# Layer 1's weight product for two graphs at a time, from seven half-size products, in a planned four-layer graph kernel

## The chip, the cores and the metric

The kernel runs on one core of one Trainium2 chip. The metric is the device time of one execution in microseconds (us). A core has a matrix engine (PE, whose weight loads are listed apart as PEld), three engines for elementwise work (DVE, ACT and POOL) and DMA queues, most of them fed by SP. Each engine takes its instructions in the order of the program and waits by semaphores for the others.

## The reference, cut to what matters

A batch of 128 graphs, each of 128 nodes with 512 features, passes four layers that share one adjacency matrix. Each layer is added to its input, and the sum is normalised.

```python
# layer 0: max over pairs of a relu, which needs only a row maximum of adj @ x
x = layernorm(x + L0(x, adj, b))
# layer 1: graph attention
h = x @ W                                  # 128x512 by 512x512
s1, s2 = h @ a1, h @ a2
e = leaky_relu(s1[:, :, None] + s2[:, None, :], 0.2) * adj
h_prime = softmax(e, axis=2) @ h
x = layernorm(x + elu(h_prime + beta * h))
# layer 2
x = layernorm(x + (adj @ x) @ W2 + bias2)
# layer 3: attention with 8 heads of 64, masked by adj == 0
q, k, v = x @ Wq + bq, x @ Wk + bk, x @ Wv + bv
x = layernorm(x + softmax(q @ k.T / 8 + mask) @ v)
```

All values are float32.

## The kernel before, in words

Work on a graph is cut into steps, and each step starts with a few matrix products. The names that the profile shows are these. `l0` multiplies by the adjacency (psA). `zT` multiplies the layer's input by the turned attention (ps_zT, L505), and `z` multiplies the result by W (ps_z, L519), which gives h_prime + beta h for one graph: four matrix products of 128x128 by 128x512 (each is two instructions in the trace). `yT` and `y` are the same for layer 2 (L560, L628). `q`, `k` and `v` are layer 3's projections for four graphs (L803), `sc` its scores (L909), `avT` or `av` the weighted sums over the values (L991, L1037).

**Seven products.** `y` takes two graphs together, and `q`, `k`, `v` take four. A product of two blocks by two blocks normally takes eight block products; Winograd's form takes seven and some sums. The sums of the weights are made once on POOL (`weight_sums`, L327). The sums of the other operand are made for each pair on POOL (`y_sums`, L576: four differences of 128x256, tile Ty). The seven products (`l2_seven`, L613) write three PSUM banks: chain, first and pair. The chain bank takes products 0, 2, 4 and 5 on top of each other; after 0, 2 and 4 ACT copies it to SBUF (tile sty, L653), POOL adds the layer's input to the copy (L657), and DVE adds the copy to the first or the pair bank (L665). Product 5 finishes the last quarter (L685). So product 2 waits for the copy after 0, product 4 for the copy after 2, product 5 for the copy after 4.

**Layer 1 before.** `l1_out` (L522) takes one graph. ACT reads the bank and computes relu(-h) and its exponential (L532, L533, tile elu_r); DVE adds the positive part and the layer's input (L536, reading PSUM) and then the exponential (L538); then comes the normalisation (`layernorm`, L351: DVE statistics at L354 and L356, three one-column operations on POOL, and one ACT pass at L365). The attention (`attention`, L458) adds s1 to s2 (L462), takes max(0.2 e, e) (L464), multiplies by adj (L465) and takes the row maximum (L467), all on DVE, and the exponential on ACT (L471). `l0` adds the bias to its maximum and takes the relu on DVE (L409).

**The order.** No scheduler runs later: the class `Plan` (L23) writes out the order while the program is built. It keeps a model of each engine. A step has a place (a priority), a cost on PE, marks that it waits for and buffers that it needs. Whenever PE is free in the model, the ready step with the lowest place is taken. The work behind a step is written as a generator: `yield dve(us)` means that the next instructions take that long on DVE, and the plan puts them into the program in the order in which its model reaches them. HOP (L20) is the model's time for a signal from one engine to the next. `sb_bufs` (L167) holds how many buffers each tile has, and `turns` (L1067) how many graphs a step runs behind `l0`. There are six PSUM banks of 512 columns (mm) and one double bank for scores (sc).

**Turned weights.** Layer 3's softmax weights are turned through a DMA round trip: written out (L376), read back into tile turn_pr (L380), and finished by a DVE transpose (L387). Two buffers (pT) hold the read-back tiles, one of which the weighted sum `avT` reads. The last six graphs are turned on PE (`pT`, L960).

## Time and profile before

| what | value |
|---|---|
| runs | 2715.48 us median of 3 (2715.01 to 2718.81) |
| profiled execution | 2713.79 us |
| its span | 2712.0 us |
| mean granted clock of PE | 0.994 |
| instructions | 45528 |
| DMA traffic | 392.42 MB, mean 145 GB/s |

The profile comes from one execution. Its own time is 1.8 us above the span of its instructions and 1.7 us below the median of the runs. An engine's busy time is the union of its instructions; a group's time is the sum of its own, and neighbours on one engine can overlap by some tens of ns. In rows of groups the columns are: line, engine, operation, output<-inputs, shapes, count, busy us, mean ns of one, and the idle time of the engine just before them with what ended it. In timelines the columns are: start, us, engine, line, operation, tiles, shapes, count. The duration of a matmul includes its way through the array, so the distance between starts says how long PE is taken.

### The profile page before, as it was taken

The numbers are of one execution on the slowest core, as the hardware profiler recorded it, in microseconds if no ns is written. First come the engines' busy times: TensorE is split into PE (matmuls) and PEld (weight loads), VectorE is DVE, ScalarE is ACT, GpSimd is POOL, SyncE is SP. The second block draws the span as 40 slices with busy tenths as digits, with TensorE's granted clock in tenths as the row PEclk, the third lists the DMA queues.
The fourth block names the chain that finished last, engine by engine and source line by source line (L and its number), as shares of the span: only waits on it lengthen the run. The fifth ranks groups of instructions, "written<-read, shape, count | busy, mean of one in ns | idle before, by whom it ended". The sixth has DMA issues, their size and how long they took to land.

```text
span 2712.0 us, 45528 instructions
## 1 busy us (share of the span) xinstructions
PE 2653.9 (98%) x14673; PEld 2076.4 (77%) x14673; DVE 2234.2 (82%) x4417; ACT 1694.8 (62%) x4381; POOL 1710.9 (63%) x2644
## 2 busy tenths in 40 slices
PE   5899999999999999999999999999999999999997
PEld 2677777777777777777777777777777777777786
DVE  7668888888888888888888888888888888888766
ACT  3446666666666666666666666666666666666655
POOL 4745566666666665666665766656666656666655
PEclk8999999999999999999999999999999999999999
DMA  3124545445545454455455455455455445454453
GB/s 126 53 61 142 150 138 161 153 144 153 157 141 152 147 157 154 141 159 158 138 160 158 131 166 151 142 161 154 143 154 159 145 147 159 143 162 137 146 158 128
DMA packets 459807, 392.42 MB, mean 145 GB/s; under 512 B 88752, under 2 KB 376624, under 8 KB 459568
## 3 DMA queue, kind: packets, MB, share of 16 engines
q1 hardware_dynamic: 456464, 383.74, 46.3%
q10 hardware_dynamic: 2976, 5.77, 0.6%
q8 instruction: 115, 1.88, 0.3%
q14 instruction: 124, 1.02, 0.1%
q0 software_dynamic: 128, 0.01, 0.0%
HBM read 218.17 MB, written 171.24 MB: 144 GB/s over the span
## 4 chain that ended last, share of the span: by engine, by line
PE 93%; DVE 2%; POOL 2%; issue 1%; ACT 0%; DMA 0%; SPq 0%; POOLq 0%; DVEq 0%; ACTq 0%
PE ps_z L519 15%; PE ps_k_chain L803 8%; PE ps_q_chain L803 8%; PE ps_y_chain L628 8%; PE ps_v_chain L803 8%; PE ps_sc L909 5%; PE ps_zT L505 4%; PE ps_av L991 4%; PE ps_yT L560 4%; PE ps_k_pair L803 4%; PE ps_y_pair L628 4%; PE ps_v_pair L803 4%; PE ps_q_pair L803 4%; PE psA L404 4%; PE ps_v_first L803 2%; PE ps_q_first L803 2%
## 5 line engine op out<-in xcount | busy, mean ns | idle before, releaser
L519 PE MATMUL ps_z<-w_sb,zT 128*128 128x512 f32 x1024 | 461.4, 593 | 2.1 <-ACT zT L511 2.1
L941 ACT ACTIVATE pr<-pr,nm 128x128 f32<-128x128 f32 x992 | 386.2, 392 | 51.9 <-DVE nm L937 24.6
L519 PEld LDWEIGHTS ps_z<-w_sb,zT 128*128 128x128 f32 x1024 | 193.6, 190 | 195.7 <-issue 183.7
L359 POOL TENSOR_SCALAR ve<-mv 128x1 f32<-128x1 f32 x512 | 118.0, 231 | 331.2 <-DVE mv L356 281.5
L361 POOL TENSOR_TENSOR rstd<-ve,nhalf 128x1 f32<-128x1 f32 x512 | 292.6, 571 | 42.6
L354 DVE BATCH_NORM_STATS2 stats<-xp 128x6 f32<-128x512 f32 x384 | 258.3, 673 | 49.8 <-POOL xp L1017 41.2
L657 POOL TENSOR_TENSOR sty<-sty,x 128x256 f32<-128x256 f32 x192 | 147.7, 769 | 222.4 <-ACT sty L653 203.6
L755 POOL TENSOR_TENSOR x3r<-x3r,bv_bc 128x512 f32<-128x512 f32 x128 | 174.8, 1366 | 162.5 <-DMA x3r<-turn_hbm_x 154.9
L365 ACT ACTIVATE xp<-xp,nmr,rstd 128x512 f32<-128x512 f32 x256 | 206.5, 810 | 94.0 <-POOL nmr L363 82.4
L420 DVE SCALAR_TENSOR_TENSOR x<-x,wa_bc 128x512 f32<-128x512 f32 x256 | 223.9, 875 | 29.0 <-ACT x L365 25.8
L551 POOL TENSOR_TENSOR x<-x,bias_bc 128x512 f32<-128x512 f32 x128 | 165.3, 1291 | 89.9 <-PE ps_yT L560 64.6
L941 ACT ACTIVATION_READ_ACCUMULATOR pr<-pr,nm 128x1 f32 x976 | 184.6, 189 | 0.0
L363 POOL TENSOR_SCALAR nmr<-mv,rstd 128x1 f32<-128x1 f32 x512 | 142.7, 279 | 53.0
L909 PEld LDWEIGHTS ps_sc<-kTh,qTh 64*128 64x128 f32 x2048 | 124.2, 187 | 64.6 <-issue 58.5
L1003 ACT COPY oT<-ps_av 128x512 f32<-128x512 f32 x122 | 133.2, 1092 | 55.3 <-PE ps_av L991 53.2
L1016 POOL TENSOR_TENSOR xp<-xp,rd 128x512 f32<-128x512 f32 x122 | 127.1, 1042 | 62.2 <-DVE xp L391 34.4
L532 ACT ACTIVATE elu_r<-ps_z 128x512 f32<-128x512 f32 x128 | 76.1, 594 | 137.2 <-PE ps_z L519 136.9
L1017 POOL TENSOR_TENSOR xp<-xp,x3r 128x512 f32<-128x512 f32 x122 | 155.6, 1276 | 9.6
L387 DVE STREAM_TRANSPOSE turn_pr<-turn_pr 128x1024 f32<-128x1024 f32 x122 | 150.7, 1235 | 13.1 <-DMA turn_pr<-turn_hbm_pr 12.9
L391 DVE STREAM_TRANSPOSE xTh<-turn_x 128x512 f32<-128x512 f32 x124 | 137.4, 1108 | 25.6 <-DMA turn_x<-turn_hbm_x 25.6
L560 PEld LDWEIGHTS ps_yT<-adjT,x 128*128 128x128 f32 x1024 | 130.3, 191 | 34.4 <-ACT x L365 17.9
L407 DVE TENSOR_REDUCE mx<-psA 128x1 f32<-128x512 f32 x128 | 87.8, 686 | 82.9 <-PE psA L404 82.7
(171 smaller groups left out, 7110.3 us busy)
## 6 DMA issues: line engine op xcount, KB each, us to landing
turn_hbm_pr<-pr SPq DMA_DIRECT2D x122, 512.0 KB
turn_pr<-turn_hbm_pr SPq DMA_DIRECT2D x122, 512.0 KB
x<-in_x_dram SPq DMA_DIRECT2D x128, 256.0 KB
out_dram<-xp SPq DMA_DIRECT2D x128, 256.0 KB
turn_hbm_x<-xp SPq DMA_DIRECT2D x124, 256.0 KB
turn_x<-turn_hbm_x SPq DMA_DIRECT2D x124, 256.0 KB
x3r<-turn_hbm_x SPq DMA_DIRECT2D x124, 256.0 KB
turn_hbm_o<-oT SPq DMA_DIRECT2D x122, 256.0 KB
```

Of the source, the lines that this page charges most:

```text
L354: nc.vector.bn_stats(stats, src)
L361: nc.gpsimd.tensor_tensor(rstd, ve, nhalf, ALU.pow)
L365: nc.scalar.activation(dst, src, AF.Identity, bias=nmr, scale=rstd)
L420: nc.vector.scalar_tensor_tensor(xin_b, x1, 1.0, wa_bc[i], ALU.mult, ALU.mult, accum_out=col)
L519: nc.tensor.matmul(ps, lhsT(c), rhs(c), start=(c == 0), stop=(c == NCC - 1))
L551: nc.gpsimd.tensor_tensor(x2, x2, bias2_bc, ALU.add)
L560: nc.tensor.matmul(ps[:, c * P : (c + 1) * P], x2[:, c * P : (c + 1) * P], adjT, start=True, stop=True)
L628: nc.tensor.matmul(ps, x_k[:, k], sums["y"][w_i][:, k, :], start=fresh and k == 0, stop=k == 1, skip_group_check=not fresh)
L755: nc.gpsimd.tensor_tensor(s["x3r"], s["x3r"], by_block(b, bv_bc), ALU.add)
L803: nc.tensor.matmul(ps[:, m, :], lhsT, rhs, start=fresh and m + k == 0, stop=m + k == 2, skip_group_check=not fresh)
L909: nc.tensor.matmul(ps[:, h % 2, f, :], heads["q", g][j // 2][r : r + HD, f, j % 2 * P : (j % 2 + 1) * P], heads["k", g][j // 2][r : r + HD ...
L941: nc.scalar.activation(pr_h[:, i], pr_h[:, i], AF.Exp, bias=nm[:, i : i + 1], accum_out=None if late else den[:, i : i + 1])
```

## The change

The change does four things. Layer 1's product z takes two graphs together, by the seven products that y has; the code of `y_sums` and `l2_seven` becomes common to both (`turned`, `pair_products`). The copies of z's chain bank go to ACT without the addition on POOL, and the fourth quarter is copied by ACT as well; the sum goes to an SBUF tile, from which the exponential linear unit is computed, in place of the bank. The leaky relu becomes one ACT operation (Prelu with a bias), and so does the bias and relu in `l0`. There is one buffer less for the turned weights. The plan gets other times: DVE and ACT operations take 0.09 and 0.1 us less of their engine, and the result comes that much later; HOP is 0.2; several single costs change. The first product of a pair or of a group of four now also asks that three banks are free, and the second that two are. The steps from yT on stand two graphs further behind `l0`.

```diff
-HOP = 0.15
+HOP = 0.2
...
-        "x0": 2, "x1": 4, "x2": 4, "x3r": 1, "xp": 4,
-        "s2_bc": 2, "s2_row": 2, "e": 2, "pe": 2, "att": 1, "attT": 2, "zT": 1, "yT": 1, "Ty": 1, "elu_r": 1,
-        "xTh": 3, "T": 1, "st": 4, "sty": 3, "qTh": 3, "kTh": 3, "pr": 1, "pT": 2, "oT": 1,
+        "x0": 2, "x1": 5, "x2": 4, "x3r": 1, "xp": 4,
+        "s2_bc": 2, "s2_row": 2, "e": 2, "pe": 2, "att": 1, "attT": 2, "zyT": 2, "Tzy": 1,
+        "xTh": 3, "T": 1, "st": 3, "stzy": 2, "qTh": 3, "kTh": 3, "pr": 1, "pT": 1, "oT": 1,
...
     def dve(us):
-        return ("DVE", us, 0.0)
+        return ("DVE", us - 0.09, 0.09)
     def act(us):
-        return ("ACT", us, 0.0)
+        return ("ACT", us - 0.1, 0.1)
...
-        rl = small.tile([P, 1], F32, tag="rl", name=f"rl_{b}")
-        nc.vector.tensor_scalar(rl, mx, b0_col, 0.0, ALU.add, ALU.max)
         plan.give("mm")
-        yield act(0.72)
+        yield act(0.95)
+        rl = small.tile([P, 1], F32, tag="rl", bufs=3, name=f"rl_{b}")
+        nc.scalar.activation(rl, mx, AF.Relu, bias=b0_col)
...
-        yield dve(1.35)
-        nc.vector.tensor_scalar(e, s2_bc, s.pop("s1"), None, ALU.add)
+        yield act(0.4)
+        nc.scalar.activation(e, s2_bc, AF.Prelu, bias=s.pop("s1"), alpha=ALPHA)
         plan.give(tag)
-        nc.vector.scalar_tensor_tensor(e, e, ALPHA, e, ALU.mult, ALU.max)
+        yield dve(0.63)
         nc.vector.tensor_tensor(e, e, adj_sb, ALU.mult)
...
+    def turned(n, b, ps):
+        p, j = divmod(b, 2)
+        if j == 0:
+            pairs[n, p] = {"T": sb_tile("zyT", [P, 2, NCC, P], f"{n}T_{p}")}
+        d = pairs[n, p]
+        yield act(0.6)
+        nc.scalar.copy(d["T"][:, j], ps.rearrange("p (c n) -> p c n", c=NCC))
+        plan.give("mm")
+        plan.mark((f"{n}T", b))
+        if j == 0:
+            return
+        t = yield from get("Tzy", [P, 3, 2, P], f"T{n}_{p}")
...
+        for i, dst, x_, y_ in ((0, t[:, 0], b12, b11), (1, t[:, 1], b22, t[:, 0]), (2, b12, b22, b12), (3, t[:, 2], b21, t[:, 1])):
+            yield pool(0.8)
+            nc.gpsimd.tensor_tensor(dst, x_, y_, ALU.subtract)
+            plan.mark((f"T{n}", p, i))
...
-        ps = product(f"z_{b}", lambda c: zT[:, c * P : (c + 1) * P], lambda c: w1_sb[:, c, :])
...
+    def l1_seven(t):
+        p, i, d = pair_products("z", t)
...
+        def temp():
+            d["st", i] = yield from get("stzy", [P, HALF], f"stz_{p}_{i}")
+            yield act(0.37)
+            nc.scalar.copy(d["st", i], d["chain"])
+            plan.mark(("z", p, i))
+
+        def finish(j, r, key):
+            yield ("mark", ("z", p, key))
+            yield dve(0.42)
+            nc.vector.tensor_tensor(half(j, r), d["first" if i == 1 else "pair"], d.pop(("st", key)), ALU.add)
...
+        elif i == 5:
+            yield ("mark", ("z", p, "C", 1, 1))
+            yield act(0.37)
+            nc.scalar.copy(half(1, 0), d["chain"])
+            plan.give("mm")
+            yield from l1_rest(2 * p + 1)
...
+        nc.scalar.activation(x2, xp, AF.Relu, scale=-1.0)
+        nc.scalar.activation(x2, x2, AF.Exp, scale=-1.0)
+        yield dve(1.5)
+        nc.vector.scalar_tensor_tensor(xp, xp, 0.0, s.pop("x1"), ALU.max, ALU.add)
+        nc.vector.scalar_tensor_tensor(xp, x2, -1.0, xp, ALU.add, ALU.add)
...
+    def bank(t):
+        i = t % 7
+        return {"mm": 1 if i in (0, 1, 3) else 0, "mm+": {0: 3, 1: 2}.get(i, 0)}
...
-    turns = {"av": 15.5, "sc": 12.5, "yT": 3, "y": 3, "l0": 0, "zT": 2, "z": 2}
+    turns = {"av": 17.5, "sc": 14.5, "yT": 5, "y": 5, "l0": 0, "zT": 2, "z": 2}
...
-        "z": (place("z"), 3.45, lambda b: [("zT", b)], need("mm"), l1_out),
+        "z": (pair_place("z"), 0.88, pair_waits("z"), bank, l1_seven),
...
-    for n, w in (("y", w2_sb), ("q", wq_sb), ("k", wk_sb), ("v", wv_sb)):
+    for n, w in (("z", w1_sb), ("y", w2_sb), ("q", wq_sb), ("k", wk_sb), ("v", wv_sb)):
         plan.at(0.0, weight_sums(n, w))
```

## The prediction

> **What bounds the kernel now.** I read the page's busy shares first, then its 40 slices, then the chain that ended last, then the costliest groups.
>
> ```profile
> span 2712.0 us, 45528 instructions
> PE 2653.9 (98%) x14673; PEld 2076.4 (77%) x14673; DVE 2234.2 (82%) x4417; ACT 1694.8 (62%) x4381; POOL 1710.9 (63%) x2644
> ...
> PE   5899999999999999999999999999999999999997
> ...
> PE 93%; DVE 2%; POOL 2%; issue 1%; ACT 0%; DMA 0%; SPq 0%; POOLq 0%; DVEq 0%; ACTq 0%
> PE ps_z L519 15%; PE ps_k_chain L803 8%; PE ps_q_chain L803 8%; PE ps_y_chain L628 8%; PE ps_v_chain L803 8%; PE ps_sc L909 5%; PE ps_zT L505 4%; PE ps_av L991 4%; PE ps_yT L560 4%; PE ps_k_pair L803 4%; PE ps_y_pair L628 4%; PE ps_v_pair L803 4%; PE ps_q_pair L803 4%; PE psA L404 4%; PE ps_v_first L803 2%; PE ps_q_first L803 2%
> ...
> L519 PE MATMUL ps_z<-w_sb,zT 128*128 128x512 f32 x1024 | 461.4, 593 | 2.1 <-ACT zT L511 2.1
> ```
>
> The reader is to see that PE is busy from the second slice to the last, that the chain which sets the end runs on PE for 93% of the span, and that the product which the change replaces, ps_z, is its longest piece. A busy PE need not be a bounding PE, so the busy time by stretches comes next (columns: length; busy time and instructions of PE, weight load, DVE, ACT, POOL; granted clock; DMA share; GB/s).
>
> ```profile
> 0.00:68.00 68.00, 38.20 (x119) 19.48 (x119) 48.58 (x125) 25.22 (x47) 32.92 (x49) 0.87 0.39 126
> 68.00:200.00 132.00, 123.89 (x568) 95.31 (x569) 89.00 (x202) 63.72 (x136) 81.73 (x127) 0.99 0.19 54
> 200.00:800.00 600.00, 598.96 (x3337) 468.77 (x3337) 507.31 (x994) 385.69 (x1005) 375.19 (x587) 1.00 0.49 150
> ...
> 2600.00:2712.00 112.00, 94.03 (x675) 81.87 (x673) 71.66 (x116) 60.94 (x168) 62.88 (x87) 0.95 0.45 143
> ```
>
> Between 200 and 2600 us PE is idle for 2 us in all at a clock of 1.00. DVE, next in line, is busy 84%. There the time is the number of PE's issue slots times their length, which PE's timeline gives as the distance between starts:
>
> ```profile
> 1010.99 3.60 PE L519 MATMUL ps_z<-w_sb,zT 128*128 128x512 f32 x8
> 1014.42 1.89 PE L803 MATMUL ps_q_chain<-T,sums_q 128*128 128x256 f32 x8
> 1016.15 1.03 PE L628 MATMUL ps_y_chain<-sums_y,Ty 128*128 128x256 f32 x4
> 1017.01 1.03 PE L628 MATMUL ps_y_pair<-w_sb,yT 128*128 128x256 f32 x4
> 1017.88 1.89 PE L803 MATMUL ps_k_chain<-T,sums_k 128*128 128x256 f32 x8
> ```
>
> One whole product z takes 1014.42 - 1010.99 = 3.43 us of PE. One of y's seven half-size products takes 0.86 to 0.87 us, and 8 such instructions 1.73, so I use 0.865.
>
> **The change on PE.** Two graphs of z now take 2 x 3.43 = 6.86 us. Afterwards they take seven products of y's kind, 7 x 0.865 = 6.055. That is 0.805 us for a pair and 64 x 0.805 = **51.5 us** in all. No other PE work changes in amount. Scores and the weighted sums over values, whose neighbours cost about 0.1 us more at each change of tiling, still stand side by side in the changed program's order on PE (380 changes of tiling against 379).
>
> **What pays for it on the other engines.** Every added operation has a twin in the y step or near it.
> - POOL: the four differences of a pair are y's row L584 once more, 106.0 + 51.5 + 49.4 = 207 us, and four weight sums of 1.3 us. POOL goes from 1711 to about 1923 us, 72% of a 2665 us span.
> - DVE loses L462, L464 and L409, 58.9 + 1.4 + 64.8 + 27.4 = 152 us. It gains the 192 additions of z, as y's L665: 52.8 + 27.0 = 80 us. L536 read PSUM at 676 ns and now reads SBUF; its neighbour L538, both inputs in SBUF, takes 821, so 0 to 145 ns x 128 = 0 to 19 us more. Net 54 to 73 us less: 2161 to 2180, 82% of the shorter span, as before.
> - ACT gains 192 copies of z as L653 (70 us), 64 copies of the fourth quarter (367 ns each: 23 us), 128 leaky relus of 128x128 with a bias (lower row: L495's copy, 259 ns; upper: L471's exp, 392: 33 to 50 us, I take 50), 128 one-column relus (from L941's 189 ns accumulator read to L828's 468: 24 to 60 us, I take 36), and 38 ns on each L532, which now reads SBUF like L533 (5 us). About 184 us, bounds 155 to 208: 1695 becomes 1880, 71%.
>
> None of these reaches PE's 98%, so the work itself hides beside PE. If that cover went, each term would count in full; POOL's is the largest.
>
> One place where a row and the notes bear on this is the lock between POOL and DVE. L464 took 291 ns at its shortest, 506 on average and 1378 at its longest, L465 485 on average, and L462, with a single input, 205 to 1354: the longest is about one POOL operation. The Trainium skill, "GPSIMD Engine Reference", Specifications, says that GpSimd shares its SBUF interfaces with DVE and that they contend when DVE has two SBUF inputs or runs a two-port mode; by this rule 207 us more of POOL makes DVE's remaining operations longer, which speaks against the change. By the rows: DVE's waits of about 0.2 us stood at POOL 63%; at 72% they grow by a seventh, 0.03 us on some 7 such operations a graph, 27 us of DVE. Two of the waiting operations go (their waits are in the 152 above). So DVE does not get fuller by it.
>
> A second rule speaks against the leaky relu on ACT. The rows: DVE spends 0.475 + 0.506 us on it and ACT's dearest like row is 0.392. "ScalarE: Activation LUTs", Rules for kernel authors, wants relu on VectorE, and under What ACT_TABLE_LOAD costs it gives about 2.66 us for each switch of table set, which for two switches a graph would be 681 us of ACT. The trace has one load of 1.28 us in the whole run; 256 such loads would be 328 us, and ACT would reach 83%. The changed program still holds a single table load, so I count none.
>
> **Waits.** The engines run in order, so a hand-off that comes late stalls all of PE. A z step 2 writes the chain bank, ACT copies it, step 4 adds to the same bank, and so on to step 5. The need is 0.165 us (a matmul's 380 ns less its 216 ns slot), a copy of 0.37, and two signals of 0.03 (the first copy of y, at 51.60 us, began 0.03 after its product ended at 51.57): 0.6 us. In the new PE order 35 of the z hand-offs and 21 of y's have just one half-size product between them, 0.865 us, so 0.27 to spare; before, 14 of y's had that. The old run lost 0.5 us of PE, and 1.7 of its weight loads, to these copies. Behind a late copy stand ACT's softmax exps (0.58 us each with the accumulator read) and oT (1.09); PE waits for all of it. At 0 to 0.3 us a tight hand-off I get 0 to 17 us; I take 4.
>
> The differences after zT need 0.58 + 2 x 0.73 us; at least 8 us of PE work stands between. z to the next yT had 6.9 us at least and now has 11. Scores follow k's last step after 4.5 us instead of 24.6, and need one DVE addition of 0.68. One buffer of turned weights instead of two: the load cannot start before the last weighted sum has ended. At 1006.39, 1024.58, 1048.97 and 1067.57 us loads were issued, and their turns on DVE started 6.3, 7.3, 7.3 and 4.6 us later; with the issue of 0.44 and the turn of 1.24, 6 to 9 us. The PE work between two weighted sums is 15.9 us at the median, and under 10 in three cases: 0 to 3 us, I take 1. No DMA is added on SP; the turned loads queue there behind others only when that sum is late.
>
> The plan's shorter costs change only the order. Its DVE costs add up to 18.6 us a graph before and 16.2 now; the trace has 507.31 us in 600, which is 17.2 a graph of 20.3 us (ps_z starts in the chain, four graphs apart: 1011.15 and 1092.20). The old plan kept DVE too full on paper, the new one too empty, so DVE can arrive late by a few per cent of a burst.
>
> **Ends.** In the first 200 us PE idles 38 us. Before, the first layer 3 product started at 97.81 us, with 50.4 us of PE slots ahead of it in the order; now 44.5 us stand there, and its pair waits for both graphs, but the second attention no longer waits behind a 3.43 us product. Bounds -10 to +10, I take 0. At the end fewer slots stand after the last scores (10.4 us, before 18.5), so PE may wait there for the softmax; but fewer outputs then pile up in the 14.4 us after PE's last matmul (2697.6 to 2712): -5 to +5, I take 0.
>
> **Sum.** From the profiled execution's 2713.8 us (span 2712.0): - 51.5 + 4 + 1 = 2667.3. The median of the runs, 2715.5, is 1.7 above that execution, so **2669 us**.
>
> **Rivals.**
> - Gain partly given back, 2680 to 2710, middle 2692: DVE's late bursts cost PE 0.4 us a pair, 64 x 0.4 = 26 us, half the gain. For it: the plan's 16.2 against 17.2. Against it: 16% of DVE's time is free, and most distances grew.
> - Slower: the hand-off from ACT becomes PE's wait. If the copies come late by one oT and one copy, 1.09 + 0.37 = 1.46 us, the 56 tight hand-offs lose 1.19 each and the 85 with two products between them (1.13 to spare) 0.33: 95 us, so 2715.5 - 51.5 + 95 = **2759**. It decides from about 1.15 us of lateness; at one oT alone it is 56 x 0.82 = 46 us and no gain is left. Against it: the old run had the same hand-offs and lost under 3 us.
> - The change doesn't do what it says: seven 256-column products cost as much as two whole ones, 0.98 us each, so 2715 to 2722. Against it: y's and q's rows.
> - More than the slots: the start runs shorter by up to 10 us and no hand-off waits, 2650 to 2658.
>
> **How the numbers follow.** Forecast 2658 to 2680: 0.62. Half given back: 0.17. Shorter start: 0.08. No gain, within 0.2% (5.4 us, about what a measurement can tell from no change): 0.04. Slower: 0.09. Faster 0.62 + 0.17 + 0.08 = 0.87. The range 2650 to 2696 leaves out the slower cases, no gain, and the upper part of the second: about 0.2.
>
> **What would show it.** Right: ps_z groups of 128x256 at 380 ns, x1792 in all; PE idle under 10 us between 200 us and 100 us before the end; about 19.9 us a graph; POOL 72%, ACT 71%, DVE 82%. Wrong: rows of waiting on PE for the z copy on ACT, for Tz on POOL or for the additions on DVE, tens of us in all; or an opening without PE work longer than 40 us.

## The result, and the profile after

The changed kernel takes **2792.13 us** (median of 4 runs, 2790.26 to 2794.36) against 2715.24 of the kernel before on the same chip (median of 4). The ratio is **1.0283, 95% interval 1.0265 to 1.0300**: slower by some 77 us, where 46 us less was forecast. The runs below were made on several chips, and each ratio is taken to the kernel before on the same one; that kernel's medians lie between 2715.2 and 2717.3 us, so differences between times of two chips are good to some 2 us. The lines of its page that answer to those of before:

```profile
span 2789.5 us, 48120 instructions
PE 2649.8 (95%) x15441; PEld 2228.5 (80%) x15441; DVE 2208.9 (79%) x4225; ACT 1828.3 (66%) x4893; POOL 1992.5 (71%) x2904
...
PE   5899999999999999999999999999999999999998
...
PE 41%; DVE 24%; POOL 23%; issue 6%; DMA 3%; ACT 2%; SPq 0%; DVEq 0%; POOLq 0%; ACTq 0%
PE ps_z_chain L563 5%; POOL rstd L367 4%; PE ps_k_chain L843 4%; DVE stats L360 3%; PE ps_q_chain L843 3%; PE ps_k_pair L843 3%; DVE xp L646 3%; PE ps_z_pair L563 3%; PE ps_v_chain L843 3%; PE ps_y_chain L563 3%; DVE xp L647 2%; POOL xp L1061 2%; PE ps_q_pair L843 2%; POOL nmr L369 2%; DVE x L426 2%
```

PE looks as busy in the slices, and its share has fallen only from 98 to 95%. The chain tells more: before, 93% of it ran on PE; now PE has 41%, DVE 24% and POOL 23%. The end is set by work that goes to and fro between three engines. The stretches (columns as before: busy time and instructions of PE, weight load, DVE, ACT, POOL; granted clock; DMA share; GB/s):

```profile
0.00:68.00 68.00, 37.33 (x117) 23.12 (x118) 45.20 (x101) 26.45 (x56) 33.76 (x52) 0.80 0.36 122
68.00:200.00 132.00, 119.33 (x574) 97.64 (x573) 90.54 (x197) 70.00 (x152) 92.27 (x137) 0.96 0.21 54
200.00:800.00 600.00, 583.61 (x3425) 492.92 (x3424) 488.09 (x937) 408.07 (x1110) 435.92 (x632) 1.00 0.48 144
...
2600.00:2789.50 189.50, 174.28 (x1137) 151.21 (x1135) 126.13 (x202) 109.03 (x288) 119.36 (x166) 0.95 0.47 146
```

From 200 to 800 us PE is idle for 16.4 us, before for 1.0. Over 200 to 2600 us it is 2400 - 2318.9 = 81 us, before 2.3, at about the same rate in each 400 us and at a clock of 0.99 to 1.00, so neither the ends (the first 200 us have 43 us of idle PE, before 38) nor the clock do it. The products themselves are as short as forecast. The timeline of PE (start, duration):

```profile
1001.00 1.03 PE L563 MATMUL ps_z_chain<-sums_z,Tz 128*128 128x256 f32 x4
1001.86 1.03 PE L563 MATMUL ps_y_chain<-w_sb,yT 128*128 128x256 f32 x4
1002.72 1.03 PE L563 MATMUL ps_z_chain<-sums_z,zT 128*128 128x256 f32 x4
...
1009.66 1.03 PE L563 MATMUL ps_y_chain<-sums_y,Ty 128*128 128x256 f32 x4
1011.59 1.13 PE L563 MATMUL ps_y_pair<-w_sb,yT 128*128 128x256 f32 x4 [0.90 <-POOL yT L533]
1012.56 1.03 PE L563 MATMUL ps_y_chain<-sums_y,Ty 128*128 128x256 f32 x4
```

Half-size products of z start 0.86 us apart, and their six groups count 512 + 5 x 256 = 1792 instructions at 379 to 391 ns (with the idle time before them and its releasers):

```profile
L563 PE MATMUL ps_z_chain<-sums_z,Tz 128*128 128x256 f32 x512 | 134.8, 386 | 5.1 <-POOL Tz L533 3.3 <-ACT stz L604 1.6
L563 PE MATMUL ps_z_pair<-w_sb,zT 128*128 128x256 f32 x256 | 68.2, 389 | 10.1 <-POOL zT L533 9.9
L563 PE MATMUL ps_z_first<-w_sb,zT 128*128 128x256 f32 x256 | 65.7, 379 | 0.0
```

Over the whole run the median distance between starts is 216 ns for these instructions and 429 ns for the 1024 of ps_z before, so a pair of graphs takes 28 x 0.216 = 6.05 us of slots in place of 16 x 0.429 = 6.86. So the 51.5 us of issue slots did go, and 77 + 51.5 = **129 us** came in, 2 us for each pair of graphs. In the profile 82 of them are idle time of PE over the whole span (139.7 us, before 58.1); most of the rest stands in its busy time, which fell by 4 us and not by 51.5. The timeline shows one place: the y pair at 1011.59 starts 1.93 us after its neighbour, with 0.90 us of waiting for a difference on POOL. PE's waits by what ended them:

```profile
engine line waited for: us in total, times, longest us
PE ps_y_pair L563 <- DVE xp L721: 26.6, 21, 2.3
PE ps_y_chain L563 <- POOL Ty L533: 15.0, 17, 2.6
PE ps_z_pair L563 <- POOL zT L533: 9.9, 11, 1.2
PE ps_z_pair L563 <- DVE s_row L446: 9.0, 8, 1.6
...
PE ps_z_chain L563 <- ACT stz L604: 6.7, 5, 5.1
```

There is no single large row. PE waits a microsecond here and there for DVE's additions and for POOL's differences, in y as much as in the new z; for ACT's copies of z it waits 6.7 us, 5.1 of it in one case. What got longer stands on DVE (busy us, mean ns, idle before):

```profile
L647 DVE SCALAR_TENSOR_TENSOR xp<-x,xp 128x512 f32<-128x512 f32 x128 | 132.1, 1032 | 13.7 <-ACT st_k L868 0.5
L646 DVE SCALAR_TENSOR_TENSOR xp<-xp,x 128x512 f32<-128x512 f32 x128 | 127.6, 997 | 0.0
...
L610 DVE TENSOR_TENSOR xp<-ps_z_pair,stz 128x256 f32<-128x256 f32 x128 | 53.1, 415 | 70.4 <-PE ps_z_pair L563 56.8 <-ACT stz L604 13.6
```

L646 and L647 are the two additions of the elu. Before, they were L536 and L538 at 676 and 821 ns; now they take 997 and 1032. That is 68 us more of DVE, where 0 to 19 were forecast. L610, the new addition of half the columns with one operand in PSUM, takes 0.41 us, as its twin L665 did before. The timeline of DVE and POOL side by side shows where the time goes (start, duration, engine):

```profile
1511.52 0.73 POOL L533 TENSOR_TENSOR Ty<-yT 128x256 f32<-128x256 f32 x1
...
1511.75 1.05 DVE L646 SCALAR_TENSOR_TENSOR xp<-xp,x 128x512 f32<-128x512 f32 x1
...
1512.91 0.69 DVE L647 SCALAR_TENSOR_TENSOR xp<-x,xp 128x512 f32<-128x512 f32 x1
...
1514.98 0.68 DVE L646 SCALAR_TENSOR_TENSOR xp<-xp,x 128x512 f32<-128x512 f32 x1
1515.04 1.21 POOL L533 TENSOR_TENSOR yT<-yT 128x256 f32<-128x256 f32 x1
...
1515.77 1.03 DVE L647 SCALAR_TENSOR_TENSOR xp<-x,xp 128x512 f32<-128x512 f32 x1
```

POOL's difference runs from 1511.52 to 1512.25. L646 is issued into it at 1511.75 and ends at 1512.80, 0.55 us after POOL has finished; L647 then meets only a one-column operation and takes 0.69. The next L646 (1514.98) is first: it takes 0.68, and it is POOL's difference issued at 1515.04 that takes 1.21 instead of 0.73. L647 at 1515.77 stands behind that one and takes 1.03. Whoever comes second waits until the other has ended. That holds for nearly all of them: of the 171 times that L646 or L647 starts under a large difference or addition of POOL (between 200 and 2600 us), 157 end 0.54 to 0.56 us after POOL's operation has ended, however long they had stood; of 61 cases of L473, with 128 columns, 52 end 0.14 to 0.16 us after it. L610, with an operand in PSUM, shows no such distance.

Sorting the instructions that the timelines list singly between 200 and 2500 or 2600 us by what ran on POOL meanwhile (large: POOL's operations on two tensors of 256 or 512 columns) gives mean ns, with the number in brackets:

| kernel, line | operands of the DVE operation | beside none or a one-column one | under a large one |
|---|---|---|---|
| before L536 | PSUM, SBUF | 683 (81) | 658 (36) |
| before L538 | both SBUF | 690 (71) | 998 (46) |
| after L646 | both SBUF | 664 (26) | 1093 (88) |
| after L647 | both SBUF | 690 (28) | 1150 (86) |
| after L426 | both SBUF | 683 (102) | 1045 (128) |
| after L473, 128x128 | both SBUF | 269 (49) | 650 (65) |
| after L610, 128x256 | PSUM, SBUF | 410 (54) | 411 (116) |

In this table only operations with both operands in SBUF are longer, by 0.3 to 0.5 us on average, and that does not go by their size: they wait for what is left of POOL's operation. In the kernel before, L465 (128x128, both in SBUF) went from 292 to 989 ns likewise; so did L462, which reads one SBUF tensor and a column, from 264 to 837, so two tensors in SBUF are not the only case. POOL pays as well: its differences of the changed kernel take 726 ns (228) alone and 982 (226) beside such an operation. And L647, which follows on L538, meets a large one in 86 of 114 cases, where L538 did in 46 of 117.

The Trainium skill, "SBUF — State Buffer", section Who interferes with whom, states this: a DVE instruction with two SBUF inputs contends with a GpSimd instruction that reads SBUF, the first to issue keeps the shared pair for its whole length, and the other is blocked. For POOL's operations on two tensors of 256 or 512 columns the trace agrees, as the distances of 0.55 us show. For its one-column operations it does not: L426 takes 683 ns beside them and 683 beside none. The prediction had drawn on another page of the skill and took the wait for a small average.

### The profile page after: what moved, and what is told of

Same layout as the page of the kernel before. It is cut to its first block, busy times and chain, and to the rows that moved or that the text cites. A ratio compares the mean times of both kernels' runs of the same rounds, so it can differ in the third digit from the quotient of the medians.

```text
span 2789.5 us, 48120 instructions
## 1 busy us (share of the span) xinstructions
PE 2649.8 (95%) x15441; PEld 2228.5 (80%) x15441; DVE 2208.9 (79%) x4225; ACT 1828.3 (66%) x4893; POOL 1992.5 (71%) x2904
## 4 chain that ended last, share of the span: by engine, by line
PE 41%; DVE 24%; POOL 23%; issue 6%; DMA 3%; ACT 2%; SPq 0%; DVEq 0%; POOLq 0%; ACTq 0%
PE ps_z_chain L563 5%; POOL rstd L367 4%; PE ps_k_chain L843 4%; DVE stats L360 3%; PE ps_q_chain L843 3%; PE ps_k_pair L843 3%; DVE xp L646 3%; PE ps_z_pair L563 3%; PE ps_v_chain L843 3%; PE ps_y_chain L563 3%; DVE xp L647 2%; POOL xp L1061 2%; PE ps_q_pair L843 2%; POOL nmr L369 2%; DVE x L426 2%
## 5 line engine op out<-in xcount | busy, mean ns | idle before, releaser
L367 POOL TENSOR_TENSOR rstd<-ve,nhalf 128x1 f32<-128x1 f32 x512 | 307.2, 600 | 42.6
L365 POOL TENSOR_SCALAR ve<-mv 128x1 f32<-128x1 f32 x512 | 134.6, 263 | 273.2 <-DVE mv L362 225.5
L426 DVE SCALAR_TENSOR_TENSOR x<-x,wa_bc 128x512 f32<-128x512 f32 x256 | 228.6, 894 | 79.5 <-ACT x L371 78.2
L369 POOL TENSOR_SCALAR nmr<-mv,rstd 128x1 f32<-128x1 f32 x512 | 154.9, 303 | 53.0
L974 DVE TENSOR_TENSOR pr<-ps_sc,mask 128x1024 f32<-128x1024 f32 x124 | 150.2, 1211 | 28.5 <-PE ps_sc L952 24.6
L952 PE MATMUL ps_sc<-kTh,qTh 64*128 64x128 f32 x2048 | 149.0, 285 | 4.2 <-DVE pr L974 4.2
L563 PE MATMUL ps_y_chain<-sums_y,Ty 128*128 128x256 f32 x512 | 134.6, 386 | 16.4 <-POOL Ty L533 15.0
L665 PEld LDWEIGHTS ps_yT<-adjT,x 128*128 128x128 f32 x1024 | 134.6, 195 | 18.8 <-ACT x L371 11.4
L980 DVE TENSOR_REDUCE nm<-pr 128x8 f32<-128x1024 f32 x124 | 148.1, 1195 | 0.3
L542 PEld LDWEIGHTS ps_zT<-attT,x 128*128 128x128 f32 x1024 | 134.1, 193 | 16.8 <-issue 4.1
```

What stands on the lines that cost most here:

```text
L367: nc.gpsimd.tensor_tensor(rstd, ve, nhalf, ALU.pow)
L369: nc.gpsimd.tensor_scalar(nmr, mv[:, 0:1], rstd, -1.0, ALU.mult, ALU.mult)
L426: nc.vector.scalar_tensor_tensor(xin_b, x1, 1.0, wa_bc[i], ALU.mult, ALU.mult, accum_out=col)
L563: nc.tensor.matmul(d[BANKS[i]], x_k[:, k], sums[n][w_i][:, k, :], start=fresh and k == 0, stop=k == 1, skip_group_check=not fresh,)
```

## The experiments

Theories at the start: **P**, the plan's prices are too short and its order too hopeful; **B**, a buffer is missing; **C**, DVE and POOL stand for each other, and the elu's additions, moved from PSUM to SBUF, make the loop longer.

**The plan's shorter times undone in the changed kernel.**
```diff
-        return ("DVE", us - 0.09, 0.09)
+        return ("DVE", us, 0.0)
...
-        return ("ACT", us - 0.1, 0.1)
+        return ("ACT", us, 0.0)
```


> The changed kernel, with only DVE's and ACT's times in the plan put back (an operation keeps its engine for its whole cost; nothing lands later). The work is the same to the instruction, only the order differs. Theory P (the plan's times): the changed plan gives DVE 2068 us of work, the trace of the changed kernel has 2209, so every engine comes later than the order assumes and PE waits; with DVE at 2342 us in the plan the waits go, and the time falls to 2680 to 2740 us. Theory C (contention): the elu's two additions took 997 and 1032 ns, where the kernel before had 676 and 821, and POOL has 200 us more, so the loop itself is longer whatever the order: 2770 us or more. Theory B (buffers: one turned tile, three q/k/v copies, two copies shared by z and y): no better than 2770 either.

Measured 2795.22 us, ratio 1.0294 (1.0279 to 1.0309). PE's wait for Ty on POOL became the largest (36.3 us, 18 times), that for the additions of y fell to 3.7. The waits move, the time does not: the general shortening alone is not the cause.

**The new times alone, in the kernel before.**
```diff
-HOP = 0.15
+HOP = 0.2
...
-        return ("DVE", us, 0.0)
+        return ("DVE", us - 0.09, 0.09)
...
-        return ("ACT", us, 0.0)
+        return ("ACT", us - 0.1, 0.1)
...
-            yield act(0.06)
+            yield act(0.16)
```


> The kernel before, with only the shorter times of the plan (DVE 0.09 and ACT 0.1 us less, landing later, and a signal of 0.2 us). Theory P: this plan gives DVE 2130 us where the trace of before has 2234, 5% too little (6% in the changed kernel), so PE should wait here as well: 2735 to 2790 us. Theories C and B: the work and the buffers are those of before, so 2705 to 2725 us.

Measured 2727.43 us, 1.0046 (1.0031 to 1.0061): 12 us, a small true cost. It lies between the two expectations: less than P asked for, and 2 us more than C and B allowed.

**One price, that of the elu's additions, in the changed kernel.**
```diff
-        yield dve(1.5)
+        yield dve(2.1)
         nc.vector.scalar_tensor_tensor(xp, xp, 0.0, s.pop("x1"), ALU.max, ALU.add)
```


> The changed kernel, with one number of the plan changed: the two additions of layer 1's elu cost 2.1 us, near the 997 + 1032 ns that they took, in place of 1.5. Theory P: these are the operations that the plan has most wrong, 0.6 us a graph, about half of DVE's missing 141 us, so a good part of the loss goes: 2710 to 2760 us. Theory C or B: the same as the changed kernel, 2780 to 2800 us.

Measured 2748.40 us, 1.0114 (1.0098 to 1.0131): 44 us better with the same work, inside the range of P. The two additions are as slow as before (945 and 1086 ns, together 2.03 us), so these 44 us did not come from shorter additions: the order left room for them.

**One buffer of turned weights, alone, in the kernel before.**
```diff
-        "xTh": 3, "T": 1, "st": 4, "sty": 3, "qTh": 3, "kTh": 3, "pr": 1, "pT": 2, "oT": 1,
+        "xTh": 3, "T": 1, "st": 4, "sty": 3, "qTh": 3, "kTh": 3, "pr": 1, "pT": 1, "oT": 1,
```


> The kernel before, with one buffer of turned softmax weights in place of two, and nothing else. Theory B: the load that can only start after the last weighted sum makes PE wait, 2740 us or more. Theories P and C: the plan knows of it and moves the weighted sums, 2712 to 2735 us.

Measured 2730.48 us, 1.0055 (1.0040 to 1.0070): 15 us, where the prediction had 1; theory B had asked for 2740 us or more.

**Relu and leaky relu on ACT, alone, in the kernel before.**
```diff
...
-        nc.vector.tensor_scalar(rl, mx, b0_col, 0.0, ALU.add, ALU.max)
...
+        nc.scalar.activation(rl, mx, AF.Relu, bias=b0_col)
...
-        nc.vector.tensor_scalar(e, s2_bc, s.pop("s1"), None, ALU.add)
...
+        nc.scalar.activation(e, s2_bc, AF.Prelu, bias=s.pop("s1"), alpha=ALPHA)
...
-        nc.vector.scalar_tensor_tensor(e, e, ALPHA, e, ALU.mult, ALU.max)
...
```


> The kernel before with the leaky relu as one ACT operation and the relu of the column maximum on ACT, and nothing else of the change (the plan's prices for these jobs as the change has them). VectorE loses some 119 us by the plan (2386 to 2267), ACT gains some 80; the plan's clock ends at 2712.7 against 2714.2. PE is at work all through the middle of the kernel before, so with no stall to remove and none made: 2705 to 2718, ratio 0.996 to 1.001. If ACT, further back in its queue, is late with the copies that the products wait for, PE's waits on ACT grow and it ends above 2721.

Measured 2717.53 us, 1.0005 (0.9995 to 1.0014). DVE's busy time falls from 2234 to 2094 us and the time stays: no gain and no harm.

**Nine prices as measured, in the changed kernel** (among them):
```diff
-        yield dve(1.5)
+        yield dve(2.1)
...
-            yield pool(0.8)
+            yield pool(0.86)
...
-        yield pool(1.09)
+        yield pool(1.15)
```


> The changed kernel, complete, with nine of the plan's prices set to what its own profile measured: elu additions 1.5 to 2.1, the scoring product L426 0.82 to 0.95, the edge multiply and maximum 0.63 to 0.72, the attention scaling 0.66 to 0.74, GpSimd's differences 0.8 to 0.86, its addition to the partial products of layer 2 0.72 to 0.82, its normalization part 1.09 to 1.15, its bias 1.28 to 1.36. With these the plan's own clock ends at 2717 us, against 2673 with the old prices and 2680 with the elu price alone. Theory P (orders fail by the prices that are wrong, and true prices would give an order that the chip keeps): the chip ends within 10 to 30 us of the plan's clock, 2727 to 2747, and PE's waits in the middle are those of the plan, some 30 us. If prices are only noise to the order and the loop is too long in itself, it stays at 2745 to 2795.

Measured 2770.60 us, 1.0201 (1.0185 to 1.0216): 22 us better than the change, and 22 worse than with one price. It missed what P expected: true averages do not make an order that the chip keeps. P, as a matter of all prices, falls as the main cause; but single prices still move the time by tens of us, so part of the loss is in how little slack an order leaves for operations that take longer than planned.

**Half-width elu, in the change's own order.**
```diff
-        nc.vector.scalar_tensor_tensor(xp, xp, 0.0, s.pop("x1"), ALU.max, ALU.add)
-        nc.vector.scalar_tensor_tensor(xp, x2, -1.0, xp, ALU.add, ALU.add)
+        nc.vector.scalar_tensor_tensor(xp[:, :HALF], xp[:, :HALF], 0.0, s.pop("x1")[:, :HALF], ALU.max, ALU.add)
+        nc.vector.scalar_tensor_tensor(xp[:, :HALF], x2[:, :HALF], -1.0, xp[:, :HALF], ALU.add, ALU.add)
```


> The changed kernel in its own order, with the two elu additions (L646, L647) on the left 256 of 512 columns; it leaves out the elu and the residual of the right half, so its numbers are not the reference's. The plan's prices and so the order of every engine are untouched: only durations change. The two take 997 and 1032 ns in the changed kernel; at half the width I expect 450 to 600 ns each, together 2.03 down to about 1.05 us, close to and below the 1.5 us that the plan gives them. Theory D (the additions end later than the plan believes, VectorE is late for all that stands behind them, and PE waits): most of the 77 us between 2792 and the 2715 of before comes back and some of the planned gain with it, 2680 to 2735. Theory G (GpSimd's differences and their one buffer set the loop, VectorE's lateness only follows): at most 25 us, 2767 or more.

Measured 2731.29 us, 1.0053 (1.0037 to 1.0069): 61 us back, inside the range of D. The rows of DVE:

```profile
L647 DVE SCALAR_TENSOR_TENSOR xp<-x,xp 128x256 f32<-128x256 f32 x128 | 97.9, 765 | 13.6 <-ACT x L644 0.6
L646 DVE SCALAR_TENSOR_TENSOR xp<-xp,x 128x256 f32<-128x256 f32 x128 | 97.0, 757 | 0.0
```

The reader is to see that half the columns still take 765 and 757 ns and not the 450 to 600 expected. L646 takes 397 ns beside none or a one-column operation of POOL (27 cases) and 867 under a large one (90): the wait of 0.47 us stays when the work is halved.

**POOL's differences as copies, in the change's own order.**
```diff
-            nc.gpsimd.tensor_tensor(dst, x_, y_, ALU.subtract)
+            nc.gpsimd.tensor_copy(dst, x_)
```


> The changed kernel in its own order, with the four GpSimd differences of each pair of graphs in layers 1 and 2 (L533) made single-input copies of the first operand; the products are then of wrong blocks and the output is not the reference's. The differences take 755 to 985 ns now, 512 of them, some 430 us of GpSimd; no row here shows a 128x256 copy on GpSimd, so I bound it between the 271 ns of a 128x1 operation and the 755 ns of today. Theory G: with 100 us or more off GpSimd in the same places PE's waits on Ty, Tz and zT (15.0, 23.1, 18.3 and 9.9 us by row) go, and 40 to 100 us come back: 2690 to 2750. Theory D: GpSimd's share falls but the additions on VectorE are still late, 2767 or more. A third theory, C (the two engines slow each other at the memory they share): the additions at L646 and L647 themselves get shorter than 997 and 1032 ns by 100 ns or more, and the time falls by some 20 to 40 us with them.

Measured 2720.18 us, 1.0010 (1.0000 to 1.0020): 72 us back. The rows of POOL, then of DVE:

```profile
L533 POOL COPY Ty<-yT 128x256 f32<-128x256 f32 x192 | 107.3, 569 | 17.6 <-PE ps_z_pair L563 17.4
L533 POOL COPY Tz<-zT 128x256 f32<-128x256 f32 x192 | 90.0, 474 | 27.5 <-ACT zT L523 13.6 <-PE ps_z_pair L563 12.4 <-PE ps_y_pair L563 1.4
```

```profile
L646 DVE SCALAR_TENSOR_TENSOR xp<-xp,x 128x512 f32<-128x512 f32 x128 | 112.2, 877 | 0.0
L647 DVE SCALAR_TENSOR_TENSOR xp<-x,xp 128x512 f32<-128x512 f32 x128 | 111.0, 868 | 13.7 <-DVE xp L646 0.5
```

POOL's operations fall from 755 to 985 ns to some 470 to 580, and DVE's additions, which nobody touched, from 997 and 1032 to 877 and 868. That is C's mark. But the time fell by more than C's 20 to 40 us, within the range of G: the copies also make POOL's own work shorter (0.39 us alone, a difference 0.73), so this run does not tell the two apart. Since each of the two last runs gives back most of the loss, neither engine is "the" late one.

**Both at once.** The edits of the last two together.


> The changed kernel in its own order with both earlier reliefs at once: the elu additions on the left 256 of 512 columns (elu and residual of the right half left out) and the GpSimd differences as copies of their first operand (products of wrong blocks). Alone they gave back 61 and 72 of the 77 us. If they are two views of one cause (the two engines standing for each other), together they give little more than one: 2700 to 2718. If they are two causes, VectorE late and GpSimd late, that add up: 2665 to 2690, the planned time of 2667 to 2673 plus what is left.

Measured 2686.79 us, 0.9894 (0.9879 to 0.9910). 105 us come back, of 61 + 72 = 133: mostly two amounts that add up, with some overlap. That is in the range given for two causes; as both edits shorten the work itself beside the waits, it does not weigh the waits alone. At this order, with its two copy buffers, 2687 us can be had once both are shorter; the forecast had been 2669.

**The elu's values in PSUM.** A test of C that keeps all the work: relu and exp are written to the product bank that has just been read, so that each addition has one operand in PSUM. The price of the pair and the time that a bank is held change with it, and so does the order on every engine.
```diff
...
-        nc.scalar.activation(x2, xp, AF.Relu, scale=-1.0)
-        nc.scalar.activation(x2, x2, AF.Exp, scale=-1.0)
-        yield dve(1.5)
-        nc.vector.scalar_tensor_tensor(xp, xp, 0.0, s.pop("x1"), ALU.max, ALU.add)
-        nc.vector.scalar_tensor_tensor(xp, x2, -1.0, xp, ALU.add, ALU.add)
+        nc.scalar.activation(r, xp, AF.Relu, scale=-1.0)
+        nc.scalar.activation(r, r, AF.Exp, scale=-1.0)
+        yield dve(1.4)
+        nc.vector.scalar_tensor_tensor(r, r, -1.0, s.pop("x1"), ALU.add, ALU.add)
+        nc.vector.scalar_tensor_tensor(xp, xp, 0.0, r, ALU.max, ALU.add)
+        plan.give("mm")
...
```


> The changed kernel, complete, with the elu's helper values in PSUM: the relu and the exp of each graph are written to the product bank that has just been read out (the bank is given back only after the additions), and the two additions become (exp - 1) + x1 in that bank and max(z, 0) + bank. So each of the two VectorE additions has one operand in PSUM, as L610 has; in the changed kernel's trace the 128x256 additions with a PSUM operand (L610, L721) take 411 and 405 ns under a large GpSimd operation and 408 and 420 ns without one, while L646 and L647, both operands in SBUF, take 1093 and 1150 ns under one and 664 and 690 ns beside small ones. The plan's price for the pair is 1.4 in place of 1.5 and its clock ends at 2687 us (2673 in the change). Theory C (a VectorE operation with both operands in SBUF stands until GpSimd's two-tensor operation is done): both rows fall to 660 to 720 ns, VectorE loses some 80 us, GpSimd's differences get shorter too, PE's waits go, and the time falls to 2695 to 2725. Rival R (the loop of copies, differences and finishes is too tight in itself, whoever is late): the rows fall but the time stays above 2745, all the more since a bank is held some 3 us longer.

Measured 2711.75 us, 0.9981 (0.9971 to 0.9990): 80 us back, and all of the loss against before. That is inside the range of C; R had asked for more than 2745. The rows of DVE (L644 has a second group of 64, on the chain bank, as L645 has):

```profile
L644 DVE SCALAR_TENSOR_TENSOR ps_z_pair<-ps_z_pair,x 128x512 f32<-128x512 f32 x64 | 44.5, 695 | 0.0
L645 DVE SCALAR_TENSOR_TENSOR xp<-xp,ps_z_pair 128x512 f32<-128x512 f32 x64 | 44.0, 688 | 2.2
```

Both take 0.69 us, under a large operation of POOL (95 cases of L645: 690) as beside none or a small one (19 cases: 690).

**The freed memory used**: x2 from 4 tiles to 3, and the half-width copies from 2 to 3.
```diff
-        "x0": 2, "x1": 5, "x2": 4, "x3r": 1, "xp": 4,
+        "x0": 2, "x1": 5, "x2": 3, "x3r": 1, "xp": 4,
...
-        "xTh": 3, "T": 1, "st": 3, "stzy": 2, "qTh": 3, "kTh": 3, "pr": 1, "pT": 1, "oT": 1,
+        "xTh": 3, "T": 1, "st": 3, "stzy": 3, "qTh": 3, "kTh": 3, "pr": 1, "pT": 1, "oT": 1,
```


> As the run before, and with the 2 KB a partition that this sets free used: the x2 tiles, no longer held by the elu, go from 4 to 3, and the half-width copies that the additions of both layers read (stzy) from 2 to 3. Complete. The plan's clock ends at 2676 us and has no wait of PE between 200 and 2500 us (2687 with 16 us of waits in the run before). Theory C with buffers as the second limit: 8 to 20 us better than the run before, 2680 to 2710, and so below the kernel before. If the buffers are no limit on the chip: within 5 us of the run before.

Measured 2681.35 us, **0.9873 (0.9859 to 0.9888)**: faster than both kernels, by 35 us than the one before on that chip, and 30 us better than the run before it, where 8 to 20 were expected. Its page:

```profile
span 2677.7 us, 47927 instructions
PE 2611.5 (98%) x15441; PEld 2225.2 (83%) x15441; DVE 2154.1 (80%) x4225; ACT 1817.8 (68%) x4893; POOL 1896.2 (71%) x2904
...
PE 84%; DVE 7%; POOL 4%; issue 2%; ACT 2%; DMA 1%; SPq 0%; POOLq 0%; DVEq 0%; ACTq 0%
```

The chain is back on PE, with 84%. Between 200 and 2600 us PE is idle for 8 us, and the same 15441 instructions take 2611.5 us of busy time, 38 less than in the changed kernel: some of that kernel's "busy" PE was stretched around waits.

**The same without the third copy buffer.**
```diff
-        "xTh": 3, "T": 1, "st": 3, "stzy": 3, "qTh": 3, "kTh": 3, "pr": 1, "pT": 1, "oT": 1,
+        "xTh": 3, "T": 1, "st": 3, "stzy": 2, "qTh": 3, "kTh": 3, "pr": 1, "pT": 1, "oT": 1,
```


> As the run that ended at 2681 us but with stzy back at 2 buffers: elu values in PSUM, x2 tiles 3, the freed memory unused. The plan's clock ends at 2686 us (2687 with four x2 tiles, 2676 with the third stzy buffer). If the third buffer for the half-width copies is what gave the last 30 us, this ends where the run with PSUM alone did, 2705 to 2718; if it was the order that came out of it, or the earlier return of x2, 2680 to 2700.

Measured 2709.70 us, 0.9970 (0.9959 to 0.9980). With the third buffer, and the order that the plan makes of it, the time is 28 us lower; the plan's clock had 10. As PE's order differs too, the run does not say how much is the buffer alone. Fewer x2 tiles change nothing clear of noise (0.9970 against 0.9981, and the intervals overlap).

**One addition back in SBUF, with every order, price and buffer of the 2681 us kernel kept.** The runs with PSUM had another order and another price, and a price alone had moved 44 us; this one changes the place of one operand.
```diff
-        nc.vector.scalar_tensor_tensor(r, r, -1.0, s.pop("x1"), ALU.add, ALU.add)
-        nc.vector.scalar_tensor_tensor(xp, xp, 0.0, r, ALU.max, ALU.add)
+        x1 = s.pop("x1")
+        nc.vector.scalar_tensor_tensor(x1, r, -1.0, x1, ALU.add, ALU.add)
+        nc.vector.scalar_tensor_tensor(xp, xp, 0.0, x1, ALU.max, ALU.add)
```


> The kernel that ended at 2681 us with one thing changed: the first elu addition writes its sum over the x1 tile in SBUF, not over the bank, so the second addition has both operands in SBUF again. Nothing else differs: the order of every engine, the prices, the buffers and the moment at which the plan gives the bank back are the same. Theory C: the second addition goes from 690 ns back to 1000 to 1150, 40 to 55 us of VectorE in all, and the time rises by 15 to 45 us, to 2696 to 2726. Rival O (the two runs with PSUM gained by another order and another price, and the place of the operands is a small matter): the row gets longer but the time stays within 8 us, 2674 to 2690.

Measured 2708.81 us, 0.9976 (0.9966 to 0.9985): 27 us worse than 2681.35, with PE's 15441 instructions in the same order in both traces. The rows of DVE (L646 is the second addition here):

```profile
L646 DVE SCALAR_TENSOR_TENSOR xp<-xp,x 128x512 f32<-128x512 f32 x128 | 141.4, 1105 | 4.4
...
L645 DVE SCALAR_TENSOR_TENSOR x<-ps_z_chain,x 128x512 f32<-128x512 f32 x64 | 44.0, 688 | 10.4 <-ACT ps_z_chain L642 10.2
```

L646 goes from 0.69 to 1.1 us (under a large operation 1129 ns, 111 cases) and L645, still with one operand in PSUM, keeps 0.69. C holds at an unchanged order; O had allowed 2690 us at most.

## Why the prediction was wrong, point by point

- **What bounds the kernel: right for before**, with 2 us of idle PE between 200 and 2600 us, so PE's slots were what there was to gain.
- **PE, 51.5 us less: right in slots** (6.05 us a pair for 6.86). 129 us came in with it, most of them waiting.
- **The step that failed is that on the lock between POOL and DVE**: "0.03 us on some 7 such operations a graph, 27 us of DVE" and "So DVE does not get fuller by it", together with "0 to 145 ns x 128 = 0 to 19 us more" for L536. A mean wait was scaled with POOL's mean share, as if the two engines met at random. L536 had escaped the wait because its operand was in PSUM. In SBUF it waits as L538 does, and both meet a large POOL operation in three of four cases, not in the 39% of L538 before. The mean wait is 0.33 us for L646, which had none as L536, and 0.34 for L647, which had 0.13 as L538; 0.03 more was forecast. The two additions grew by 68 us. DVE ended at 2209 us, above the 2161 to 2180 given, and POOL at 1992 instead of 1923, although Tz alone (103.3 + 50.9 + 48.3 = 203) was as forecast: the 70 us are its old operations, longer (the one-column ones of the normalisation by 43 us, y's differences by 26).
- **"The work itself hides beside PE": wrong, though the shares fitted.** DVE at 79% and POOL at 71% hide nothing if they stand on the way from one product to the next: z's additions, the elu, the normalisation and the differences lie between PE steps that the plan had set as close as its prices allowed. It held 1.5 us for the elu's additions, and they take 2.03; with 2.1 held for them the loss was 33 us and not 77.
- **ACT: 1880 us forecast (1850 to 1903 by its bounds), 1828 measured.** The leaky relu took 395 ns as taken, the one-column relu 289 to 291, z's copies 70 us, the fourth quarter 24; one table load, as counted. The terms were right: the durations of all of ACT's instructions grew by 181 us, from 2002 to 2183, with 184 forecast. But 47 us more of them overlap their neighbours, and busy time counts an overlap once. The bounds were a sum of durations. Alone, the move to ACT changes nothing (1.0005).
- **Hand-offs to ACT, 4 us (0 to 17): right in size.** The slower rival rested on them and was right in its direction only: PE waited 6.7 us for z's copies, and its weight loads 12.5 for y's.
- **The number of copy buffers was not in the sum at all.** z and y share two; with the elu in PSUM a third, and the order that comes of it, is worth 28 us. The prediction priced the time of a copy, not the wait for its place. No run adds the third buffer to the changed kernel itself; with both additions and differences made shorter that kernel reached 2687 us with two, 18 above the forecast.
- **One turned buffer, 1 us (0 to 3): wrong**, 15 us alone in before. **Plan's shorter times, order only, nothing: nearly**, 12 us alone in before. Whether these two add up in the changed kernel was not tried.
- **Rival "gain partly given back", DVE's late bursts at 0.4 us a pair**: the right engine, for another reason and with the wrong size. It laid the lateness to the plan's short DVE costs (16.2 against 17.2 us a graph), and with those undone the time was 2795 us. DVE is late because its operations became longer, and all that came in is 2 us a pair.
- **The signs named beforehand** told it: 380 ns x1792 for the products, as named for right; and, as named for wrong, tens of us of PE's waiting in rows on POOL and on DVE's additions, though more of it before y's products than before z's.

Shown: DVE's additions with both operands in SBUF wait for POOL's operations, to a fixed distance from their end; one of the two, put back into SBUF at an unchanged order, costs 27 us; and 80 us come back when the additions no longer wait, though with another order. Open: how the 129 us divide among the waits, the order with no room for them (one price gives back 44 us) and the buffers, since no run takes away the waits alone in the change's own order with all the work kept; and why nine measured prices give a worse order than one. No run separates that from chance in the ordering.

## What to carry to other kernels

Before a PSUM operand of a VectorE operation is moved to SBUF, look at what GpSimd does at that moment: sort the operation's durations by what overlaps them, and don't scale a mean wait with a share of busy time. When a tight order is made tighter, the engines beside the bound one stop being free, even at 70 to 80%: price their latency from one product to the next, buffers included. And where an operand would have to move into SBUF, a bank just read out can hold it instead: here that, with the order that the plan made of it, turned 2792 us into 2712, and into 2681 with one more buffer.

## What the runs showed of the hardware

- A 128x512 DVE addition takes 0.66 to 0.71 us with an operand in PSUM, whatever POOL does, and 1.00 to 1.15 on average with both in SBUF under a large two-tensor POOL operation. The wait does not shrink with the work: 0.31 to 0.46 us at 512 columns, 0.46 to 0.47 at 256, 0.38 at 128 (L473; 0.70 for L465 before).
- Such an operation, started under POOL's, ends at a fixed time after it: 0.55 us at 512 columns (157 of 171 cases of L646 and L647 within 0.01 us), 0.28 at 256 (162 of 176, half-width elu), 0.15 at 128 (52 of 61 of L473).
- The wait goes both ways: POOL's 128x256 difference takes 726 ns alone and 982 beside such an operation.
- POOL's one-column operations do not delay DVE to be seen, long as they last (570 ns for rstd alone): L426 takes 683 ns beside them and 683 beside none. They are delayed themselves: rstd takes some 0.70 us beside a DVE operation with both operands in SBUF.
- A 128x256 copy on POOL takes 0.39 us beside no DVE operation with both operands in SBUF, and 0.47 to 0.58 on average in the run with copies; a difference of two tensors takes 0.73 alone.
